# Cross-attention on one core: five instruction groups moved in the first rounds and in the tail

## The chip, the cores and the metric

The kernel runs on one core of a Trainium2 chip. The metric is the device time of one execution in microseconds (us). Five engines work side by side, each through its own instructions in order: TensorE (PE) multiplies matrices into PSUM, VectorE (DVE), ScalarE (ACT) and GpSimd (POOL) work element by element, and SyncE (SP) issues the DMA transfers. They wait for each other by semaphores.

## The reference

For each of 64 batches, with x of 256 rows by 512 and a context c of 256 rows by 384, all in float32:

```python
text_p = einsum('bld,dh->blh', x, W_text) + b_text
audio_p = einsum('bsd,dh->bsh', c, W_audio) + b_audio
Q = layer_norm(text_p, g1, beta1)
K = layer_norm(audio_p, g2, beta2)
alpha = softmax(einsum('blh,bsh->bls', Q, K) / sqrt(512))
H = einsum('bls,bsh->blh', alpha, audio_p)
H = einsum('blh,hk->blk', H, W_out) + b_out
out = layer_norm(H + x, g_out, beta_out)
```

## The kernel before

**What is computed how.** The kernel does the value projection last: alpha times c (the context, 256 by 384) times the product W_audio W_out, which it makes once (`fold_multiply`, `fold_evict`, `fold_bias`). The projections of the rounds use schemes with fewer products than a plain multiplication, and pay for it with sums. Class `Fork` (q, line 624) takes seven products of halves of W_text (`one` to `seven`), with the sums `xsum` of x made by POOL; class `Thirds` (k, and the output product `o` of a batch, line 516) cuts the rows of the weights in thirds, with the sums `csum` and `zsum` of c and z made by POOL and the sums `wa_thirds` and `wao_thirds` of the weights made once. `third_weights` (line 356) makes the latter in parts 0 to 4; in each a few sums of 128x171, on the engine that it is given. Part 2 is four sums; two of their results are weights of the products `four` and `five` of k. The results sit in PSUM, and steps such as `after_five` (DVE: a sum from one PSUM area to another, line 671) or `after_one` (ACT: a copy, line 654) stand between products: the next product adds to what they left.

Rows are turned into columns by a trip through memory outside the core: `store` writes rows, `fetch` reads them back as squares of 32 (`squares`, four DMAs, line 69), and DVE turns the squares (`turn`). This holds for q, k and for the exponentials e: `divide_e` (ACT, two instructions, line 743), `store_e`, `fetch_e`, `turn_e`.

**Order.** Everything is issued by hand in program order (`manual_schedule`), so each engine has exactly the order in which its calls stand, and SP the order of the loads, stores and fetches. Before the loop comes a start-up, in which batches 0 and 1 are projected and the weight sums are made (lines 1030 to 1106). Line 1079 gives parts 4 and 2 of the sums to DVE between `q[1].after_six()` and `q[1].after_five()` (line 1089); then come `turn_x(2)` (line 1090) and `q[1].rest()` (line 1095).

The loop at line 1112 has rounds b = 0 to 61. Round b loads the squares of c and x of batch b + 4 (`load_c`, `load_x`), projects batch b + 2 (`k2`, `q2`), scores batch b (`at`), takes the context of batch b - 1 (`last`), the output product of batch b - 2 (`old`) and the last layer norm of batch b - 3 (`settled`). The first rounds differ from the others: round 0 has no `last`, and round 1 does the softmax of batch 0 and later also that of its own batch. At the head of round 2 stand the loads of batch 6, among them the fetch of e of batch 1, and then the two loads of g_out and beta_out (`row`, line 118: one row of 512 to all 128 partitions, 256 KB). The division of e of batch 1 stands at the end of round 1 (lines 1324 and 1325), ahead of the copies of its context (`copy_one`, line 1327, and `copy_two` in round 2).

**The tail** (lines 1330 to 1430) finishes the last batches: `settled` is batch 59, `old` 60, `last` 61, `at` 62, `end` 63. Batches 62 and 63 take the output product plainly, in two tiles of 128 rows, three matmuls of 512 columns each (`multiply`, line 855). A tile then goes through `evict` (DVE, with statistics), `scale_soon` (DVE, and a power on POOL that gives the scale `rone`), `shift` (DVE: less the mean, times g_out) and `settle` (DVE: times the scale, plus beta_out). For batch 61 and for tile 0 of batch 63 the last step is instead `scale_row` on ACT and `lift_rows` on POOL, and the statistics come from `deviations` on ACT (squares, then POOL's power gives `rstd`). Tile 1 of batch 63 goes in halves of 256 columns (`multiply_halves`, `evict_halves`, `settle_halves`), each half with its own store. All lines are those of the kernel before.

Of the kernel before, what the change touches and what calls it, by code (L numbers as in the profile page):

```python
# [15 lines left out]
P = 128  # L16
# [6 lines left out]
def kernel(  # L23
# [18 lines left out]
    nc = tc.nc  # L42
    ctx.enter_context(tc.manual_schedule())
    B, L, D = x.shape
    S, DA = c.shape[1:]
    H = w_text.shape[1]
    LT, ST = L // P, S // P
    DC, AC, HC = D // P, DA // P, H // P
# [4 lines left out]
    H2 = H // 2  # L53
# [15 lines left out]
    def squares(dst, src):  # L69

        v = src.rearrange("(b j) (q f) -> q j b f", j=SQ, q=NQ)
        for q in (0, 2, 1, 3):
            nc.sync.dma_start(dst[q * SQ : (q + 1) * SQ], v[q])
# [7 lines left out]
    def load_c(b):  # L81
        cq = blk.tile([P, S // SQ, DA // NQ], F32, tag="cq", name=f"cq_{b}")
        squares(cq, c[b])
        blocks[b] = [cq]

    def load_x(b):
        xq = blk.tile([P, L // SQ, D // NQ], F32, tag="xq", name=f"xq_{b}")
        squares(xq, x[b])
        blocks[b].append(xq)
# [40 lines left out]
    wa_sb = const.tile([P, AC, H], F32, tag="wa", name="wa")  # L130
# [87 lines left out]
    def bias_parts():  # L218

        part = once.tile([P, D], F32, tag="e", name="part")  # L220
        nc.vector.scalar_tensor_tensor(
            part, wo_sb[:, 0, :], bac_sb[:, 0:1], bo_sb, ALU.mult, ALU.add
        )
        return part
# [8 lines left out]
    wao_sb = const.tile([P, AC, D], F32, tag="wao", name="wao")  # L233
# [15 lines left out]
    def fold_evict(a):  # L249
        nc.scalar.copy(wao_sb[:, a, :], folds[a])  # L250
# [7 lines left out]
    def moments(mv, src, t):  # L258

        st = small.tile([P, 6], F32, tag="st", name="st")  # L260
        nc.vector.bn_stats(st, src)
        nc.vector.bn_aggr(mv[:, t, :], st)
# [93 lines left out]
    def third_weights(w_sb, t, parts=(0, 1), engine=nc.gpsimd):  # L356

        b = [[w_sb[:, c, j : j + W3] for j in starts] for c in range(3)]
        w = {n: t[:, i, :W3] for i, n in enumerate((10, 4, 5, 1, 6, 2, 8, 9, 0, 3, 7))}
        w.update({14: b[2][0], 13: b[1][2], 11: b[0][0], 12: b[0][2]})  # L360
        plus = lambda o, i0, i1: engine.tensor_tensor(o, i0, i1, ALU.add)
        less = lambda o, i0, i1: engine.tensor_tensor(o, i0, i1, ALU.subtract)
        if 0 in parts:
            plus(w[0], b[1][1], b[1][2])
            less(w[6], w[0], b[2][0])
            less(w[2], b[1][0], w[0])
            plus(w[0], b[0][0], b[1][0])
            less(w[8], w[2], w[0])
        if 3 in parts:
            plus(w[0], w[0], b[1][2])  # L370
            less(w[9], b[1][2], b[2][0])
            less(w[7], b[0][1], b[0][0])
            plus(w[7], w[7], b[0][2])
        if 1 in parts:
            less(w[3], b[2][1], b[2][0])
            less(w[10], w[3], b[0][2])
        if 4 in parts:
            plus(w[4], w[3], b[2][2])
            plus(w[3], b[0][2], b[2][0])
            plus(w[3], w[3], b[2][2])  # L380
        if 2 in parts:
            less(w[5], b[2][0], b[2][1])
            less(w[5], w[5], b[1][2])
            less(w[1], w[5], b[1][1])
            less(w[1], w[1], b[0][1])
        return w
# [9 lines left out]
    def rstd_of(var, n, total=False):  # L396

        ve = small.tile([P, n], F32, tag="ve", name="ve")
        if total:
            nc.gpsimd.tensor_scalar(ve, var, 1.0 / D, EPS, ALU.mult, ALU.add)  # L400
        else:
            nc.gpsimd.tensor_scalar(ve, var, EPS, None, ALU.add)
        r = small.tile([P, n], F32, tag="rstd", name="rstd")
        nc.gpsimd.tensor_tensor(r, ve, nhalf[:, :n], ALU.pow)  # L404
        return [r[:, t : t + 1] for t in range(n)]
# [289 lines left out]
    class Attention:  # L695
# [138 lines left out]
                    junk, self.y[:, t, :], AF.Identity, scale=-1.0 / D, accum_out=self.nm[:, t : t + 1]  # L834
                )

        def deviations(self, lo=0, n=LT):

            for t in self.summed:
                junk = work.tile([P, D], F32, tag="junk", name="junk")  # L840
                nc.scalar.activation(  # L841
                    junk,
                    self.y[:, t, :],
                    AF.Square,
                    bias=self.nm[:, t : t + 1],
                    accum_out=self.ssq[:, t : t + 1],
                )
            self.r = dict(zip(self.summed, rstd_of(self.ssq[:, lo : lo + n], n, total=True)))
# [48 lines left out]
        def moments(self, tiles=range(LT)):  # L897
            if 0 in tiles:
                self.mv = small.tile([P, LT, 2], F32, tag="mvy", name="mvy")
            for t in tiles:  # L900
                moments(self.mv, self.y[:, t, :], t)
            if LT - 1 in tiles:
                self.scales()

        def multiply_halves(self, t, banks):
            self.ps_h = []
# [67 lines left out]
    def turn_x(b):  # L974
        xT = work.tile([P, DC, L], F32, tag="xT", name=f"xT_{b}")
        turn(xT, blocks[b][1], DC)
        return xT
# [12 lines left out]
    q, k, xT, cT, xs, cs, att = {}, {}, {}, {}, {}, {}, {}  # L990
    bank = third + fork
# [77 lines left out]
    wa_t = const.tile([P, 11, WP], F32, tag="wa_thirds", name="wa_thirds")  # L1069
# [6 lines left out]
    fold_multiply(1, 0, 2)  # L1076
    q[1].six()
    q[1].after_six()
    third_weights(wa_sb, wa_t, [4, 2], nc.vector)
    fold_evict(0)  # L1080
    Thirds.seed_with(ba_sb)
    k[1].normalise()
# [5 lines left out]
    q[1].five()  # L1088
    q[1].after_five()
    xT[2] = turn_x(2)  # L1090
    part = bias_parts()
    bias_rest(part, 1, 3)
    folds.append(p_at.tile([P, H], F32, tag="at", name="ps_fold"))
# [18 lines left out]
    for b in range(B - 2):  # L1112
        at = att[b] = att.get(b) or Attention(b)
        settled, old, last = att.pop(b - 3, None), att.get(b - 2), att.get(b - 1)
        three = b + 3 < B
        if b + 4 < B and b != 1:
            load_c(b + 4)
            if b == 2:
                last.fetch_e()
            load_x(b + 4)  # L1120
        if b == 2:
            go_sb = row(g_out, "go")
            beo_sb = row(beta_out, "beo")
        if b == 0:
            Fork.seed()
        k2 = k[b + 2] = Thirds("k", b + 2, cs.pop(b + 2), wa_blocks, ba_sb, ba_delta)
        if b < 3:
# [46 lines left out]
        q2.after_seven()  # L1174
        if b == 1:
            last.divide_e()
        if b < 3:
            at.affine_keys()
        else:
            at.affine_keys(2, 3)  # L1180
# [139 lines left out]
            last.context_one()  # L1320
        if three and old:
            k2.seed()
        if three and b:
            at.divide_e()
            at.store_e()
        if last and three:
# [2 lines left out]
    settled, old, last = att[B - 5], att[B - 4], att[B - 3]  # L1329
    at = att[B - 2]  # L1330
# [33 lines left out]
    end = Attention(B - 1)  # L1364
# [33 lines left out]
    last.o.leave_plus(x_rows[B - 3], lambda: None)  # L1398
    end.transpose_e(bank[5])
    end.copy_e()  # L1400
    at.multiply(1, bank[4])
    at.settle(0)
    last.totals()
    last.deviations()
    at.evict(1)
    at.scale_soon(1)
    at.shift(1)
    end.context()
    last.shift(0)
    last.shift(1)  # L1410
    at.settle(1)
    at.store()
    end.start_output()
# [6 lines left out]
    end.evict(0, stats=False)  # L1420
    end.statistics(0, 1)
    end.evict_halves(1, [0])
    end.shift(0)
    end.scale_row(0)
    end.evict_halves(1, [1])
    end.scale_soon(1)
    end.lift_rows(0, 1)
    end.shift(1)
    end.settle_halves(1)
    end.store(0, 1)  # L1430


# [30 lines left out]
```

## Time and profile before

| | |
|---|---|
| time, median of 3 runs | 1371.05 us (1370.75 to 1374.13) |
| the profiled execution, its own time | 1370.49 us |
| its span, first to last instruction | 1368.7 us |
| granted TensorE clock, mean | 0.999 |
| instructions | 26400 |
| DVE busy | 1112.9 us (81%) |
| ACT busy | 1090.0 us (80%) |
| POOL busy | 1159.8 us (85%) |
| DMA | 322.02 MB, mean 235 GB/s |

How to read the views that follow. A row of the timeline has the start and the duration in us, the engine, the line of the kernel, the operation, what it writes and reads with shapes, how many instructions were merged, and in brackets for how long the engine had been idle before it and which work ended that. `SPq` is the issue of a DMA, not its transfer. A matmul in float32 shows as two instructions per product. A row of the waits has the waiting engine, tile and line, the releaser, the total in us, the number of waits and the longest. A row of the stretches has the stretch, its length, the busy time of PE, PE's weight loads, DVE, ACT and POOL with the number of instructions, the granted clock, the busy share of the DMA engines and what they moved in GB/s.

### The profile page before, as it was taken

Reading aid. Unit: us, or ns where it says so; the run is one execution under the profiler, and the core shown is the slowest. Engines: PE = TensorE matmul, PEld = TensorE weight load, DVE = VectorE, ACT = ScalarE, POOL = GpSimd, SP = SyncE. Lnnn points to the kernel's source line nnn. Section 1 sums busy time; section 2 is a strip of 40 time slices with the busy share of each in tenths; the row PEclk is TensorE's granted clock in tenths of the full one; section 3 lists DMA queues with packets and bytes.
Section 4 is the critical chain, followed back from the end, with each engine's and each line's share of the span. In section 5 each row is a group of like instructions: output and inputs, shape, how many; then the busy total and the mean of one; then the engine's idle time right before and its main releaser. Section 6 shows DMA issues by size and latency. Waiting matters only on the chain. (4 is left out here: it accounts for less than half of the span.)

```text
span 1368.7 us, 26400 instructions
## 1 busy us (share of the span) xinstructions
PE 1356.2 (99%) x7423; PEld 1239.6 (91%) x7423; DVE 1112.9 (81%) x2688; ACT 1090.0 (80%) x2689; POOL 1159.8 (85%) x1928
## 2 busy tenths in 40 slices
PE   9999999999999999999999999999999999999997
PEld 5789999999999999999999999999999999999995
DVE  6778888888888888888888888888888888888868
ACT  5678888888788788888788887887887888888884
POOL 5788888888888888888888888888888888888866
PEclk9999999999999999999999999999999999999999
DMA  9788988988887889788779888798888888798762
GB/s 218 212 230 240 264 244 237 241 246 232 250 241 239 246 238 248 224 251 245 237 238 249 235 236 250 233 236 245 245 241 239 242 251 233 237 245 228 221 221 103
DMA packets 449096, 322.02 MB, mean 235 GB/s; under 512 B 153781, under 2 KB 381621, under 8 KB 448950
## 3 DMA queue, kind: packets, MB, share of 16 engines
q1 hardware_dynamic: 448854, 320.20, 82.3%
q8 instruction: 60, 0.98, 0.3%
q14 instruction: 86, 0.70, 0.2%
q10 hardware_dynamic: 96, 0.13, 0.0%
HBM read 203.57 MB, written 116.65 MB: 234 GB/s over the span
## 5 line engine op out<-in xcount | busy, mean ns | idle before, releaser
L712 PE MATMUL ps_sc<-kT,qT 128*128 128x256 f32 x1024 | 260.9, 379 | 0.0
L340 POOL TENSOR_TENSOR zsum<-zsum,zT 128x256 f32<-128x256 f32 x305 | 191.9, 646 | 14.4
L712 PEld LDWEIGHTS ps_sc<-kT,qT 128*128 128x128 f32 x1024 | 186.3, 190 | 17.3 <-ACT zT L793 0.2
L778 PE MATMUL ps_z<-eT,c 128*128 128x256 f32 x768 | 186.2, 379 | 0.0
L644 PE MATMUL ps_f<-wtsum,xsum 128*128 128x256 f32 x756 | 184.5, 380 | 0.3 <-ACT ps_f L655 0.3
L340 POOL TENSOR_TENSOR csum<-csum,cT 128x256 f32<-128x256 f32 x310 | 173.0, 567 | 9.9
L778 PEld LDWEIGHTS ps_z<-eT,c 128*128 128x128 f32 x768 | 143.0, 190 | 17.0 <-issue 0.5
L966 POOL TENSOR_TENSOR yr<-yr,beo 128x512 f32<-128x512 f32 x122 | 153.2, 1277 | 3.4 <-ACT yr L962 3.4
L644 PEld LDWEIGHTS ps_f<-wtsum,xsum 128*128 128x128 f32 x756 | 137.9, 190 | 15.0 <-issue 0.7
L404 POOL TENSOR_TENSOR rstd<-ve,nhalf 128x2 f32<-128x2 f32 x192 | 136.7, 712 | 16.0
L340 POOL TENSOR_TENSOR zsum<-zT 128x256 f32<-128x256 f32 x122 | 73.5, 602 | 86.3 <-ACT zT L796 86.3
L505 ACT ACTIVATE qT<-qT,columns 128x256 f32<-128x256 f32 x256 | 139.1, 594 | 2.8 <-DVE qT L76 2.8
L505 ACT ACTIVATE kT<-kT,columns 128x256 f32<-128x256 f32 x256 | 139.2, 595 | 1.5 <-DVE kT L76 1.1
L644 PE MATMUL ps_f<-wt,xT 128*128 128x256 f32 x504 | 129.3, 379 | 0.0
L729 ACT ACTIVATE e<-ps_sc,nmx 128x256 f32<-128x256 f32 x128 | 59.5, 469 | 63.4 <-DVE nmx L722 63.4
L948 DVE SCALAR_TENSOR_TENSOR yr<-yr,nm,go 128x512 f32<-128x512 f32 x124 | 103.7, 838 | 0.9 <-ACT junk L841 0.9
L644 PEld LDWEIGHTS ps_f<-wt,xT 128*128 128x128 f32 x504 | 92.9, 190 | 10.5 <-issue 0.5
L514 DVE TENSOR_TENSOR ps_l<-ps_m,t 128x171 f32<-128x171 f32 x248 | 85.5, 345 | 17.0
L796 ACT COPY zT<-ps_z 128x256 f32<-128x256 f32 x64 | 23.8, 372 | 85.7 <-PE ps_z L778 85.7
L514 DVE TENSOR_TENSOR ps_f<-ps_f,s 128x256 f32<-128x256 f32 x126 | 54.4, 432 | 46.0 <-PE ps_f L644 43.3
L841 ACT ACTIVATE junk<-yr,nm 128x512 f32<-128x512 f32 x124 | 87.9, 712 | 2.8 <-POOL nm L822 2.8
L962 ACT ACTIVATE yr<-yr,rstd 128x512 f32<-128x512 f32 x122 | 87.3, 717 | 2.1 <-POOL rstd L404 1.3
(247 smaller groups left out, 3775.7 us busy)
## 6 DMA issues: line engine op xcount, KB each, us to landing
kd<-kr SPq DMA_DIRECT2D x64, 512.0 KB, 2.9
kq<-kd SPq DMA_DIRECT2D x256, 128.0 KB, 3.1
qd<-qr SPq DMA_DIRECT2D x64, 512.0 KB, 2.9
qq<-qd SPq DMA_DIRECT2D x256, 128.0 KB, 2.7
xq<-in_x_dram SPq DMA_DIRECT2D x252, 128.0 KB, 3.2
x<-in_x_dram SPq DMA_DIRECT2D x63, 512.0 KB, 4.7
out_dram<-yr SPq DMA_DIRECT2D x62, 512.0 KB, 3.9
cq<-in_ctx_dram SPq DMA_DIRECT2D x252, 96.0 KB, 3.3
```

Of the source, the lines that this page charges most:

```text
L340: nc.gpsimd.tensor_tensor(*step)
L404: nc.gpsimd.tensor_tensor(r, ve, nhalf[:, :n], ALU.pow)
L505: nc.scalar.activation(self.T[:, k, :], self.T[:, k, :], AF.Identity, bias=bet[:, k : k + 1], scale=gam[:, k : k + 1],)
L514: nc.vector.tensor_tensor(o, i0, i1, op)
L644: nc.tensor.matmul(place, lhsT=side, rhs=w, start=False, stop=True, skip_group_check=True)
L712: nc.tensor.matmul(self.sc[:, t, :], lhsT=self.q.T[:, k, bass.ts(t, P)], rhs=self.k.T[:, k, :], start=(k == 0), stop=(k == HC - 1),)
L729: nc.scalar.activation(self.e[:, t, :], self.sc[:, t, :], AF.Exp, bias=self.nmx[:, t : t + 1], accum_out=self.den[:, t : t + 1],)
L778: nc.tensor.matmul(ps, lhsT=c_rows[self.b][:, s, bass.ts(j, P)], rhs=self.eT[:, s, :], start=(s == 0), stop=(s == ST - 1),)
L841: nc.scalar.activation(junk, self.y[:, t, :], AF.Square, bias=self.nm[:, t : t + 1], accum_out=self.ssq[:, t : t + 1],)
L948: nc.vector.scalar_tensor_tensor(row, row, self.nm[:, t : t + 1], go_sb, ALU.add, ALU.mult)
L962: nc.scalar.mul(self.y[:, t, :], self.y[:, t, :], self.r[t])
L966: nc.gpsimd.tensor_tensor(self.y[:, t, :], self.y[:, t, :], beo_sb, ALU.add)
```

## The change

Five groups of instructions move or take another form; what is computed stays.

1. Part 2 of the weight sums stands behind `turn_x(2)` instead of ahead of `after_five`.
2. `divide_e` and `store_e` of batch 1 stand in round 2 behind `after_seven`, no longer at the end of round 1; the loads of batch 6, with the fetch of that e between them, follow them there.
3. g_out and beta_out are loaded at the head of round 0 instead of round 2.
4. In the tail the second tile of batch 62 is multiplied in halves of 256 columns (`multiply_half`, new: three matmuls each), one ahead of and one behind the context of batch 63. The copies of that context stand ahead of and between the two instructions of `last.deviations`. `last.shift(0)` stands ahead of `at.evict(1)`, `last.shift(1)` between `at.scale_soon(1)` and `at.shift(1)`.
5. At the very end tile 0 of batch 63 is shifted and settled on DVE, behind the shift of tile 1, and stored ahead of the halves of tile 1; `scale_row` and `lift_rows` of that tile are gone.

```diff
-        def deviations(self, lo=0, n=LT):
+        def deviations(self, lo=0, n=LT, between=None):
             for t in self.summed:
+                if t and between:
+                    between()
...
+        def multiply_half(self, t, bank, h):
+            self.ps_y[t] = bank
+            for k in range(AC):
+                nc.tensor.matmul(
+                    bank[:, bass.ts(h, H2)],
+                    lhsT=self.zT[:, k, bass.ts(t, P)],
+                    rhs=wao_sb[:, k, bass.ts(h, H2)],
+                    start=(h == 0 and k == 0),
+                    stop=True,
+                    skip_group_check=True,
+                )
...
-    third_weights(wa_sb, wa_t, [4, 2], nc.vector)
+    third_weights(wa_sb, wa_t, [4], nc.vector)
...
     q[1].after_five()
     xT[2] = turn_x(2)
+    third_weights(wa_sb, wa_t, [2], nc.vector)
...
-        if b + 4 < B and b != 1:
+        if b + 4 < B and b not in (1, 2):
             load_c(b + 4)
-            if b == 2:
-                last.fetch_e()
             load_x(b + 4)
-        if b == 2:
+        if b == 0:
             go_sb = row(g_out, "go")
             beo_sb = row(beta_out, "beo")
-        if b == 0:
             Fork.seed()
...
         q2.after_seven()
         if b == 1:
             last.divide_e()
+        if b == 2:
+            last.divide_e()
+            last.store_e()
+            load_c(b + 4)
+            last.fetch_e()
+            load_x(b + 4)
...
-        if three and b:
+        if three and b > 1:
             at.divide_e()
             at.store_e()
...
-    at.multiply(1, bank[4])
+    at.multiply_half(1, bank[4], 0)
     at.settle(0)
     last.totals()
-    last.deviations()
+    end.context_one()
+    end.copy_one()
+    for s in range(ST):
+        end.context_two(s)
+    last.deviations(between=end.copy_two)
+    at.multiply_half(1, bank[4], 1)
+    last.shift(0)
     at.evict(1)
     at.scale_soon(1)
+    last.shift(1)
     at.shift(1)
-    end.context()
-    last.shift(0)
-    last.shift(1)
     at.settle(1)
...
     end.evict_halves(1, [0])
-    end.shift(0)
-    end.scale_row(0)
     end.evict_halves(1, [1])
     end.scale_soon(1)
-    end.lift_rows(0, 1)
     end.shift(1)
+    end.shift(0)
+    end.settle(0)
+    end.store(0, 1)
     end.settle_halves(1)
-    end.store(0, 1)
```

## The prediction

> **What bounds the kernel now.** I read the page first, then the stretches of the span, the waits of TensorE, the chain that ended last, and the timelines around the edited places.
>
> ```profile
> PE 1356.2 (99%) x7423; PEld 1239.6 (91%) x7423; DVE 1112.9 (81%) x2688; ACT 1090.0 (80%) x2689; POOL 1159.8 (85%) x1928
> ```
>
> ```profile
> 200.00:1300.00 1100.00, 1100.00 (x6139) 1023.01 (x6138) 908.57 (x2218) 899.12 (x2221) 957.39 (x1589) 1.00 0.84 240
> ```
>
> ```profile
> PE ps_f L644 <- DVE ps_f L514: 1.3, 1, 1.3
> PE ps_m L858 <- ACT zT L793: 0.5, 1, 0.5
> ```
>
> ```profile
> 1363.09 1.47 DVE y L940
> ```
>
> PE is busy 1356.2 us of 1368.7, and all of the 1100 us between 200 and 1300 (second row, first engine column). The rounds in the middle are bound by TensorE without a gap, and they issue the same work in the same order after the change. So the change can only reach the 12.5 us in which PE is idle: waits among the first rounds (1.3 us behind DVE, and two of 0.3 and 0.2 shown below), 0.5 behind ACT in the tail, and the time behind PE's last matmul, where the chain ends on DVE's settle of the last halves. All four waits gone and a tail some 1.5 us shorter make less than 4 us. A difference of 0.3%, about what a measurement of this kernel can tell from no change, is 4.1 us.
>
> **Part 1: weight sums behind after_five and the turn of x.**
>
> ```profile
> 36.92 0.61 DVE L362 TENSOR_TENSOR wa_thirds<-wa 128x171 f32<-128x171 f32 x1
> 37.56 1.49 DVE L362 TENSOR_TENSOR wa_thirds<-wa_thirds,wa 128x171 f32<-128x171 f32 x3
> 38.97 0.42 DVE L514 TENSOR_TENSOR ps_f<-ps_f,s 128x256 f32<-128x256 f32 x1
> 49.37 0.42 DVE L514 TENSOR_TENSOR ps_f<-ps_f,bt_step 128x256 f32<-128x256 f32 x1
> ```
>
> ```profile
> 36.29 1.88 PE L241 MATMUL ps_fold<-wo,waT 128*128 128x512 f32 x4
> 39.44 1.13 PE L644 MATMUL ps_f<-wt,xsum 128*128 128x256 f32 x4 [1.27 <-DVE ps_f L514]
> 50.20 1.03 PE L644 MATMUL ps_f<-wtsum,xsum 128*128 128x256 f32 x4
> ```
>
> ```profile
> 40.00:50.00 10.00, 10.00 (x48) 7.99 (x47) 9.28 (x18) 5.83 (x14) 5.89 (x9) 1.00 0.70 205
> ```
>
> PE's product q[1].rest (39.44) waits for DVE's after_five (38.97), and ahead of that on DVE stand the four sums of part 2, from 36.92 to 38.97: 2.05 us. Behind the move after_five starts at about 36.95 and ends by 37.4; PE is through with the products at 36.29 at about 38.1. So the whole stall goes: 1.27 us idle and some 0.2 of slower issue around it, 1.45.
>
> What is late next: DVE. It has the same work as before and hardly a pause, in order, up to after_six of batch 2 (ends 49.37 + 0.42 = 49.79), and PE's product at 50.20 needs that result. In 40 to 50 DVE is busy 9.28 of 10 us, so idle 0.72, nearly all of it before 49.79. PE can come earlier there by its slack of 0.41, less 0.1 for the signal, plus 0.6 of that idle time: 0.9. The rest of the 1.45 comes back as small waits of PE at about 44 and 49. Behind 50 DVE has room (5.95 busy in 50 to 60, below), and the gain stays. The moved sums are first used by the products near 49, 8 us after they are made, and the turn of x comes earlier: nothing else waits. Bounds: 0.3, if none of DVE's idle time lies on this path, to 1.45, if its sums run faster at their new place (they took 0.50 to 0.61 each in the rows). I take 0.9, from the row of DVE's idle time.
>
> **Part 2: the division of round 1 behind the copies of round 2.**
>
> ```profile
> 76.57 1.03 PE L644 MATMUL ps_f<-wt,xT 128*128 128x256 f32 x4
> 78.74 1.10 PE L644 MATMUL ps_f<-wtsum,xsum 128*128 128x256 f32 x4 [0.28 <-ACT ps_f L655]
> ```
>
> ```profile
> 76.66 0.91 ACT L743 ACTIVATE e<-e,rden 128x256 f32<-128x256 f32 x2
> 78.19 0.41 ACT L655 COPY ps_f<-ps_f 128x256 f32<-128x256 f32 x1
> 83.64 0.30 ACT L583 COPY u<-ps_u 128x171 f32<-128x171 f32 x1 [1.81 <-PE ps_u L530]
> ```
>
> ```profile
> 81.94 0.40 SPq L747 DMA_DIRECT2D ed<-e  x1
> ```
>
> ACT did the two divisions at 76.66, then two copies of zT, then the copy of R (78.19 to 78.60), for which PE's product six waited until 78.74. With 0.91 us less ahead of it, that copy waits only for PE's product one, done at 77.60, and is over by 78.0; six follows seven at 78.3 without a wait. Gain 0.45: 0.28 idle and the slowed issue around it. The divisions come back behind the next copy, and end before 80; ACT's affines run up to 0.9 later, into the 1.81 us for which ACT sat idle before 83.64. Without that cover the copies at 83.64 would be up to 0.9 late. Queued behind the divisions on SP is the store of e; it was issued at 81.94, and so is not held up by a division that ends at 80. The loads of c and x of batch 6 and the fetch of e follow it in the same order as before. Bounds: 0.28, the idle time alone, to 0.45; I take 0.45.
>
> **Part 3: rows of g_out and beta_out loaded in round 0.**
>
> ```profile
> 52.14 1.87 SPq L73 DMA_DIRECT2D xq<-in_x_dram  x4
> 58.99 0.38 SPq L476 DMA_DIRECT2D qd<-qr  x1
> 61.85 1.84 SPq L73 DMA_DIRECT2D qq<-qd  x4
> 90.06 0.43 SPq L120 DMA_DIRECT2D beo<-in_L_xattn_beta_out_dram  x1
> 92.46 0.37 SPq L476 DMA_DIRECT2D qd<-qr  x1
> 100.30 1.81 SPq L73 DMA_DIRECT2D qq<-qd  x4
> ```
>
> ```profile
> 107.56 0.71 DVE L498 STREAM_TRANSPOSE kT<-kq 128x512 f32<-128x512 f32 x1 [0.74 <-DMA kq<-kd]
> ```
>
> ```profile
> 110.15 0.53 PE L530 MATMUL ps_u<-wao_thirds,zsum 128*128 128x171 f32 x2 [0.23 <-DVE ps_u L514]
> ```
>
> ```profile
> 50.00:60.00 10.00, 10.00 (x55) 9.15 (x54) 5.95 (x11) 9.12 (x24) 6.82 (x15) 1.00 0.56 133
> ```
>
> In round 2 the two row loads (256 KB each) stood on SP just ahead of two tile loads and the store of q (92.46). The fetch that needs this store came 7.84 us after it (100.30); in round 0 it came after 2.86 (58.99 to 61.85). Then DVE waited 0.74 us for k's squares (107.56), and behind that its sum, for which PE waited at 110.15, was late: 0.23 idle, about 0.4 with the slowed issue. At the 240 GB/s of the middle of the span, 512 KB less in front are 2.2 us, more than the 0.74: the wait goes. In round 0 the loads are issued at 54.0 (52.14 + 1.87), when SP has nothing to do until 58.99 and the DMA engines are busy at 0.56 and 133 GB/s; the same 2.2 us put them through before the store. Bounds: 0, if the wait stays, to 0.4, all of it; I take 0.4.
>
> **Part 4: the tail.** The product of batch 62's second tile goes in halves around the last context; the last batch's first tile is settled on DVE alone.
>
> ```profile
> 1348.79 2.74 PE L858 MATMUL ps_f<-wao,zT 128*128 128x512 f32 x6
> ```
>
> ```profile
> 1352.59 0.72 ACT L841 ACTIVATE junk<-yr,nm 128x512 f32<-128x512 f32 x1 [2.82 <-POOL nm L822]
> 1354.02 0.56 ACT L793 COPY zT<-ps_z 128x512 f32<-128x512 f32 x1
> ```
>
> ```profile
> 1354.80 1.41 DVE L948 SCALAR_TENSOR_TENSOR yr<-yr,nm,go 128x512 f32<-128x512 f32 x2
> 1356.65 0.75 DVE L957 SCALAR_TENSOR_TENSOR y<-y,rone,beo 128x512 f32<-128x512 f32 x1 [0.44 <-POOL rone L887]
> 1357.52 0.75 DVE L867 SCALAR_TENSOR_TENSOR y<-ps_m,rden,x 128x512 f32<-128x512 f32 x1
> 1358.81 0.48 DVE L925 SCALAR_TENSOR_TENSOR y<-ps_l,rden,x 128x256 f32<-128x256 f32 x1 [0.54 <-PE ps_l L911]
> 1359.96 0.75 DVE L948 SCALAR_TENSOR_TENSOR y<-y,nm,go 128x512 f32<-128x512 f32 x1 [0.21 <-ACT junk L841]
> 1363.09 1.86 DVE L940 SCALAR_TENSOR_TENSOR y<-y,rone,beo 128x256 f32<-128x256 f32 x2 [0.43 <-POOL rone L887]
> ```
>
> ```profile
> 1356.94 2.83 POOL L966 TENSOR_TENSOR yr<-yr,beo 128x512 f32<-128x512 f32 x2 [0.32 <-ACT yr L962]
> 1363.03 1.25 POOL L966 TENSOR_TENSOR y<-y,beo 128x512 f32<-128x512 f32 x1
> ```
>
> ```profile
> 1365.51 0.40 SPq L969 DMA_DIRECT2D out_dram<-y  x1
> ```
>
> PE does half the product (1.3 of 2.6 us), the context from 1350.1, and the other half until 1354.0. ACT copies z at 1352.0, not at 1354.02, so PE's wait of 0.5 goes. But PE does not set the end here, DVE does. It now shifts row 0 of batch 61 first, which waits for ACT's squares (1352.59 + 0.72 = 1353.31), then evicts the product at 1354.2, and after the same instructions as before (statistics, two shifts) settle(1) of batch 62 is up at 1357.35, 0.7 later than at 1356.65.
>
> There POOL comes in. Before, POOL's sum at 1356.94 waited for ACT's scaled row, and settle(1), which waits only for rone, had begun. Now row 0 is shifted by 1354.1 instead of 1355.5, ACT has scaled it by 1356.2, and POOL goes from rone straight on to the sum, ahead of settle(1). What that costs is seen at 1363.03: POOL's sum of 1.25 us began 0.06 ahead of DVE's settle, and a half that needs 0.47 took 1.47. So settle(1) ends near 1359.1, and end.evict(0) starts at 1359.05 instead of 1357.52: 1.55 later. The nearest row without such a delay is the pair of shifts at 1354.80, 0.7 each while POOL worked on its rstd; by it end.evict(0) starts at 1358.05. I go by 1363.03, where POOL's operation is the same.
>
> The Trainium skill, "SBUF — State Buffer", section "Who interferes with whom", has a rule for it: a VectorE instruction with two SBUF inputs and a GpSimd instruction that reads SBUF shut each other out, and the one that starts first keeps the port. By it settle(1) waits and the parts sum to 2.2; without it they sum to 3.2. The row at 1363.03 agrees.
>
> Behind end.evict(0) the new order is shorter. Before, the last store was issued 8.0 us after it (1357.52 to 1365.51). Out of these fall 1.0 behind POOL's sum, DVE's waits of 0.54, 0.21 and 0.43 (its three rows with brackets), and 0.55 for which the store of row 0 came after the last half (1363.09 + 1.86 = 1364.95). In comes DVE's settle(0), 0.7. That leaves 6.0, and the tail gains 8.0 - 6.0 - 1.55 = 0.45. Bounds: 1.45 without POOL's hold; -0.25 if POOL's last rone is shut out during one more whole-row operation of DVE (0.7).
>
> **The sum:** 0.9 + 0.45 + 0.4 + 0.45 = 2.2 us. The profiled execution took 1370.49 (1.8 around its span), so it would take 1368.3; the median of the runs shown, 1371.05, is 0.56 above it, so 1368.8 there, which I predict.
>
> **The rivals.**
> - POOL does not get ahead of settle(1). For: the pair at 1354.80. Against: 1363.03. The tail gives 1.45, the sum 3.2: 1367.8. Chance 0.19.
> - DVE becomes the bound of round 0 and gives most of part 1 back. For: 9.28 of 10 us busy. Against: it does have idle time. Part 1 gives 0.3, the sum 1.6: 1369.4. Chance 0.16.
> - The tail doesn't do what the edit says: end.evict(0) 1.55 late and rone shut out once more. Sum 1.5: 1369.5. Chance 0.11.
> - Slower: the row loads are still in the DMA queue when round 0 stores q. In round 2 the way from that store to its fetch was 5.0 us longer than in round 0 (7.84 against 2.86). If 61.85 comes 5 us later, the fetch of e of round 0 behind it on SP does too, and PE's first context product waits for that e: up to 5.0, less the 2.2, so 2.8 slower: 1373.8. It decides as soon as PE is held up there by over 2.2 us. Against it: 5 us of a free SP, and DMA engines at 0.56. Chance 0.08.
>
> **How the numbers follow.** The forecast has 0.46. The range goes from 1366.6 to 1371.6: the upper bounds give 1.45 + 0.45 + 0.4 + 1.45 = 3.75, so 1367.3, the lower ones 0.3 + 0.28 + 0 - 0.25 = 0.33, so 1370.7, each with 0.7 to 0.9 for the spread of the runs shown (1370.75 to 1374.13). It leaves out the last rival and little else. Faster by over 0.3% needs over 4.1 us, all upper bounds and a lucky run: 0.09. Slower by over 0.3% needs the last rival at its worst, or something not seen: 0.08. Within 0.3%: 0.83.
>
> **What would show it.** After the change: no wait of PE for after_five near 38, small ones near 44 or 49 instead; none for the copy of R near 77; no wait of DVE for k's squares near 106, and none of PE behind it; the row loads on SP near 53. In the tail settle(1) of batch 62 at 1.3 us or more beside POOL's sum, end.evict(0) later and the last store earlier (by 0.45) than before, both against the first rounds' gain. I am wrong if PE is idle past round 3, or waits for a fetch in rounds 0 and 1.

## The result, and the profile after

The changed kernel takes **1369.17 us** (median of 14 runs, 1367.89 to 1371.05) beside 1371.74 us for the kernel before in the same comparison (14 runs, 1370.60 to 1374.13): a ratio of 0.9981, 95% interval 0.9973 to 0.9989, so 2.6 us faster (1.5 to 3.7). The prediction was 1368.8, or 2.2 us less. The profiled execution took 1368.85 us (span 1367.1, mean granted clock 0.998), where the working had given 1368.3.

Busy time of each engine, from the page, and TensorE's waits, from the view of the waits:

```profile
PE 1355.5 (99%) x7429; PEld 1241.0 (91%) x7429; DVE 1113.6 (81%) x2689; ACT 1089.9 (80%) x2688; POOL 1158.6 (85%) x1927
```

```profile
PE ps_f L184 <- POOL ones L108: 1.5, 1, 1.5
PE ps_z L778 <- DVE eT L76: 1.1, 1, 1.1
```

All four waits behind DVE and ACT that the prediction counted are gone. The first row, 1.5 us, is the wait of the start-up that was there before. The second row is new.

TensorE's timeline of the first rounds shows both. This start-up is 0.28 us later than that of before (the fold product near 36 us stands at 36.57 against 36.29), so distances from that product are compared.

```profile
36.57 1.88 PE L241 MATMUL ps_fold<-wo,waT 128*128 128x512 f32 x4
38.28 1.03 PE L644 MATMUL ps_f<-wt,xsum 128*128 128x256 f32 x4
48.98 1.03 PE L644 MATMUL ps_f<-wtsum,xsum 128*128 128x256 f32 x4
72.52 1.99 PE L778 MATMUL ps_z<-eT,c 128*128 128x256 f32 x8 [1.14 <-DVE eT L76]
77.53 1.89 PE L644 MATMUL ps_f<-wtsum,xsum 128*128 128x256 f32 x8
109.33 0.45 PE L530 MATMUL ps_u<-wao_thirds,zsum 128*128 128x171 f32 x2
```

q[1].rest (38.28) follows the fold product without a gap. The product near 50 stands 12.41 us behind that fold product (48.98 - 36.57), where it was 13.91 before (50.20 - 36.29): 1.50 gained, not 0.9. Product six at 77.53 and the product at 109.33 don't wait, as forecast. But the first context product waits 1.14 us at 72.52 for e's turned squares. The place is that of the slower rival, below the 2.2 us from which that rival would have decided. But the prediction also named a wait for a fetch in rounds 0 and 1 as a sign that it is wrong. This is such a wait, in round 1, and the sum has no term for it.

DVE and POOL in that stretch, and SP:

```profile
34.93 0.33 DVE L361 TENSOR_TENSOR wa_thirds<-wa_thirds,wa 128x171 f32<-128x171 f32 x1
35.29 0.74 DVE L361 TENSOR_TENSOR wa_thirds<-wa 128x171 f32<-128x171 f32 x1
36.77 0.43 DVE L514 TENSOR_TENSOR ps_f<-ps_f,s 128x256 f32<-128x256 f32 x1
38.27 0.35 DVE L362 TENSOR_TENSOR wa_thirds<-wa 128x171 f32<-128x171 f32 x1
```

```profile
34.98 3.03 POOL L340 TENSOR_TENSOR csum<-csum,cT 128x256 f32<-128x256 f32 x5
```

```profile
54.42 0.44 SPq L120 DMA_DIRECT2D beo<-in_L_xattn_beta_out_dram  x1
57.77 0.38 SPq L476 DMA_DIRECT2D qd<-qr  x1
61.95 1.81 SPq L73 DMA_DIRECT2D qq<-qd  x4
64.36 1.92 SPq L73 DMA_DIRECT2D kq<-kd  x4
91.22 0.37 SPq L476 DMA_DIRECT2D qd<-qr  x1
97.05 1.80 SPq L73 DMA_DIRECT2D qq<-qd  x4
```

The first of the moved sums takes 0.35 us at its new place (38.27), 0.61 before; the other three 1.45 and 1.49 together. The one at 34.93 began just ahead of POOL's five sums of c (34.98 to 38.0) and took 0.33; the one at 35.29, in the midst of them, took 0.74; the moved ones stand behind them. DVE is through earlier, and none of the small waits of TensorE near 44 or 49 that the prediction expected shows here. On SP, the fetch of q in round 3 follows its store by 5.83 us (91.22 to 97.05; 7.84 before), as wanted. In round 0 it follows by 4.18 (57.77 to 61.95; 2.86 before).

The tail, against a first-round gain of 1.12 us (batch 62's first settle stands at 1350.56, before at 1351.68). The lines are the changed kernel's: L971 is `settle`, L869 `evict`, L980 `lift_rows`, L925 the last batch's halves on TensorE, L957 the stores of those halves:

```profile
1356.36 1.57 DVE L971 SCALAR_TENSOR_TENSOR y<-y,rone,beo 128x512 f32<-128x512 f32 x1
1357.86 0.74 DVE L869 SCALAR_TENSOR_TENSOR y<-ps_m,rden,x 128x512 f32<-128x512 f32 x1
```

```profile
1355.97 3.09 POOL L980 TENSOR_TENSOR yr<-yr,beo 128x512 f32<-128x512 f32 x2
```

```profile
1356.72 1.46 PE L925 MATMUL ps_u<-wao,zT 128*128 128x256 f32 x6
```

```profile
1363.38 0.87 SPq L957 DMA_DIRECT2D out_dram<-y  x2
```

Settle(1) takes 1.57 us beside POOL's sum (forecast "1.3 us or more"); end.evict(0) is 1.46 later than before once the 1.12 is taken out (forecast 1.55). The last of the two stores in the row at 1363.38 starts at about 1363.82, so 0.57 earlier in the same sense (1365.51 - 1363.82 - 1.12; forecast 0.45).

So the sum came true, with one term too small (1.50 for 0.9) and a wait of 1.14 against it. The experiments ask which of these figures belongs to the program and which to this one execution.

### The profile page after: what moved, and what is told of

The parts are those of the page before. It is cut to its first block, busy times and chain, and to the rows that moved or that the text cites. A ratio compares the mean times of both kernels' runs of the same rounds, so it can differ in the third digit from the quotient of the medians.

```text
span 1367.1 us, 26408 instructions
## 1 busy us (share of the span) xinstructions
PE 1355.5 (99%) x7429; PEld 1241.0 (91%) x7429; DVE 1113.6 (81%) x2689; ACT 1089.9 (80%) x2688; POOL 1158.6 (85%) x1927
## 5 line engine op out<-in xcount | busy, mean ns | idle before, releaser
L980 POOL TENSOR_TENSOR yr<-yr,beo 128x512 f32<-128x512 f32 x122 | 153.6, 1281 | 3.1 <-ACT yr L976 3.1
L311 POOL TENSOR_TENSOR xsum<-xT 128x256 f32<-128x256 f32 x124 | 88.2, 733 | 0.0
```

The lines of the kernel that those rows point to most:

```text
L311: self.engine.tensor_tensor(*step)
L980: nc.gpsimd.tensor_tensor(self.y[:, t, :], self.y[:, t, :], beo_sb, ALU.add)
```

## The experiments

**Theory A** for the wait at 72.5: the two row loads, now in round 0, hold up q's store and with it the fetches behind it. **Theory B**: the fetch of e is where it always was, and TensorE, 1.5 us earlier, only waits longer there. In the expectations of the first three runs below, A is the theory and B the rival. All comparisons below are with the kernel before on the same chip; differences in us are the ratio times 1371.

### Part 3 undone

```diff
         if b == 0:
-            go_sb = row(g_out, "go")
-            beo_sb = row(beta_out, "beo")
...
         if b == 2:
...
             load_x(b + 4)
+            go_sb = row(g_out, "go")
+            beo_sb = row(beta_out, "beo")
```

> The changed kernel with its part 3 undone: the two row loads (g_out, beta_out) stand in round 2 again, behind the loads of batch 6. Theory (the two loads hold up round 0's store of q, and behind it the fetches of q and e): TensorE's wait of 1.14 us for e's turned squares near 72.5 us is gone (under 0.1), the fetch of q in round 0 again follows its store by about 2.9 us instead of 4.2, and in round 3 VectorE's wait for k's squares and TensorE's stall near 110 come back (0.2 to 0.4 us). Net about 0.7 to 0.8 us faster than the changed kernel, near 1368.4 where that is 1369.2. Rival (TensorE arrives 1.5 us earlier from part 1, and the fetch of e has not moved): the wait near 72.5 stays at 0.8 us or more, and the kernel is 0.3 to 0.4 us slower than the changed one.

1370.17 us (11 runs), ratio 0.9992 (0.9983 to 1.0001): 1.1 us faster than before, not the 0.7 better than the changed kernel that theory A wanted. The fetch of q does follow its store by 2.86 us again. TensorE's timeline:

```profile
71.77 2.00 PE L778 MATMUL ps_z<-eT,c 128*128 128x256 f32 x8 [0.43 <-DVE eT L76]
109.22 0.53 PE L530 MATMUL ps_u<-wao_thirds,zsum 128*128 128x171 f32 x2 [0.48 <-DVE ps_u L514]
117.86 0.82 PE L530 MATMUL ps_n<-wa,csum 128*128 128x171 f32 x4 [0.91 <-DVE yr L614]
```

The wait for e is 0.43, between the two theories. The stall of round 3 is back, and larger than in the profile of before: 0.48 and 0.91 instead of 0.23.

### Each part alone

Part 3 alone on the kernel before (the diff's lines for `row`):

> The kernel before with part 3 alone: the two row loads in round 0. Theory (the loads hold up the fetch of e): TensorE waits for e's turned squares near 73.5 us in the kernel before's time, for 1 us if the transfer had no slack there, less by whatever slack it had; the stall of round 3 goes; net between 0.4 faster and 0.8 slower than the kernel before. Rival (the wait needs part 1's earlier TensorE): no wait near 73.5, stall of round 3 gone, 0.4 us faster.

1369.62 us (11 runs), ratio 0.9991 (0.9982 to 1.0000): 1.2 us faster. No wait for e, and no stall in round 3. Theory A's lag does not show either: the fetch of q follows its store by 2.86 us with the row loads ahead of it.

```profile
54.05 0.43 SPq L120 DMA_DIRECT2D beo<-in_L_xattn_beta_out_dram  x1
58.52 0.38 SPq L476 DMA_DIRECT2D qd<-qr  x1
61.38 2.46 SPq L73 DMA_DIRECT2D qq<-qd  x4
```

Part 1 alone (`third_weights` 2 behind `turn_x(2)`):

> The kernel before with part 1 alone: the weight sums behind the turn of x. Measured in the changed kernel's trace, TensorE is 1.5 us earlier near 50 us. Theory (the later wait for e comes from the row loads): no wait near 72, all of the 1.5 us stays, 1.45 us faster than the kernel before. Rival (the wait comes from the earlier TensorE): a wait for e near 72 of 0.8 us or more, and net under 0.7 us faster. The forecast's own figure for this part was 0.9 us, with small waits of TensorE near 44 and 49: if it holds they show here.

1370.68 us (11 runs), ratio 0.9995 (0.9987 to 1.0004): 0.7 us faster. In its trace TensorE, then DVE and POOL:

```profile
44.98 1.10 PE L255 MATMUL ps_bias<-part,ones 128*128 128x512 f32 x2 [0.61 <-DVE part L229]
72.86 1.99 PE L778 MATMUL ps_z<-eT,c 128*128 128x256 f32 x8 [0.30 <-DVE eT L76]
77.87 1.93 PE L644 MATMUL ps_f<-wtsum,xsum 128*128 128x256 f32 x8
112.21 0.53 PE L530 MATMUL ps_u<-wao_thirds,zsum 128*128 128x171 f32 x2 [2.34 <-DVE ps_u L514]
```

```profile
43.55 1.28 DVE L229 SCALAR_TENSOR_TENSOR part<-wo,columns,part 128x512 f32<-128x512 f32 x1
43.56 1.86 POOL L311 TENSOR_TENSOR xsum<-xT 128x256 f32<-128x256 f32 x2
```

Here is the small wait near 44 that the prediction expected: DVE's operation at 43.55 takes 1.28 us (0.74 at the same place in the changed kernel), TensorE waits 0.61 for it, and part 1 is worth 0.6 us up to the product near 50. Here POOL's sums of x begin together with that operation (43.56). The wait for e is 0.30: theory B wanted 0.8 or more. TensorE does not wait for the copy of R (77.87, products seven and six in one row), though the division stands where it was before. And round 3 stalls for 2.34 us.

The tail alone (points 4 and 5 of the change):

> The kernel before with the tail (parts 4 and 5 of the change) alone. Theory: the tail is 0.45 to 0.55 us shorter than before, settle of batch 62's second tile takes 1.5 us or more beside GpSimd's sum, and the eviction of the last batch's first tile comes 1.45 to 1.55 us later than before. Rival (tail worth nothing): the last store is issued within 0.2 us of before's 1365.5. Rival (the tail's 0.5 us needs the earlier first rounds): not possible with TensorE busy without a gap in between, so the same tail shows here shifted in time by 1.1 us.

1370.45 us (11 runs), ratio 0.9996 (0.9987 to 1.0005). Its rounds are those of the kernel before, and yet TensorE waits for e:

```profile
73.57 1.99 PE L778 MATMUL ps_z<-eT,c 128*128 128x256 f32 x8 [0.87 <-DVE eT L76]
```

```profile
61.94 3.06 SPq L73 DMA_DIRECT2D qq<-qd  x4
65.59 1.92 SPq L73 DMA_DIRECT2D kq<-kd  x4
```

This row shows that neither theory is the whole cause: 0.87 us of wait with neither the row loads nor the earlier TensorE. SP took 3.06 us to issue the four fetches of q, 1.84 in the profile of before, and everything behind them on SP was later. Round 3 does not stall in this execution. In the tail, with a shift of 0.13 (batch 62's first settle at 1351.81), end.evict(0) is 1.45 later and the last store some 0.58 earlier than before.

Part 2 alone (the diff's lines for `divide_e` and `store_e`, with the row loads left behind the loads of batch 6):

> The kernel before with part 2 alone: the division of round 1 behind the copies of round 2; the row loads stay in round 2 behind the loads of batch 6. Theory: TensorE's wait for the copy of R near 78.7 is gone, ScalarE's later affines hold nothing up, 0.28 to 0.45 us faster than the kernel before, too little for the time alone to show. In round 3, where the row loads still stand ahead of q's store, TensorE stalls again between 105 and 120 us, as in the kernel before and in the looks at the weight sums alone and at the changed kernel with its rows in round 2 (0.2 to 2.3 us); no stall there speaks for a mere accident. Rival (ScalarE's affines become late): a new wait of TensorE for ScalarE between 80 and 92 us.

1371.44 us (11 runs), ratio 1.0004 (0.9995 to 1.0013). TensorE does not wait for the copy of R, and ACT brings up no new wait. That alone does not show the mechanism, since TensorE came 0.66 us late, held by e; and 0.3 to 0.45 us is below what the time can show. Round 3 stalls for 2.07 us:

```profile
112.38 0.53 PE L530 MATMUL ps_u<-wao_thirds,zsum 128*128 128x171 f32 x2 [2.07 <-DVE ps_u L514]
```

### The cost doubled

Two more row loads behind the two of round 2, in the kernel before:

```diff
             beo_sb = row(beta_out, "beo")
+            row(g_out, "go2")
+            row(beta_out, "beo2")
```

> The kernel before, with the suspected cost doubled: behind the two row loads of round 2 stand two more of the same kind, into tiles that nothing reads, 512 KB more in front of q's store. Theory (the row loads hold up q's store and the fetches behind it, and TensorE stalls in round 3 for that): the fetch of q in round 3 follows its store by about 10 us instead of 7.7 to 9.1, VectorE waits 2 to 3 us for k's squares, TensorE stalls 1.5 to 3 us between 105 and 120 us, and the kernel is 1 to 2.2 us slower than the kernel before. Rival (the stall of round 3 comes from other transfers and varies by itself): the stall stays within the 0 to 2.3 us that four looks with the loads in round 2 have shown, and the time within 0.5 us of the kernel before.

**1377.12 us** (5 runs), ratio 1.0043 (1.0031 to 1.0056): 5.9 us slower, far over the 1 to 2.2 expected. SP, TensorE, and the stretches of the span (the columns after PE's: weight loads, DVE, ACT, POOL, granted clock, DMA share, GB/s):

```profile
95.03 2.21 SPq L476 DMA_DIRECT2D qd<-qr  x1
105.65 1.81 SPq L73 DMA_DIRECT2D qq<-qd  x4
```

```profile
114.67 0.91 PE L530 MATMUL ps_u<-wao_thirds,zsum 128*128 128x171 f32 x2 [4.65 <-DVE ps_u L514]
```

```profile
96.00:98.00 2.00, 2.00 (x14) 1.88 (x13) 1.90 (x8) 0.72 (x2) 0.51 (x2) 1.00 1.06 103
98.00:100.00 2.00, 2.00 (x12) 1.80 (x11) 1.64 (x4) 1.62 (x5) 1.09 (x2) 1.00 0.98 132
...
114.60:117.00 2.40, 2.33 (x6) 2.08 (x7) 1.56 (x4) 0.37 (x1) 2.24 (x4) 0.50 1.01 207
117.00:120.00 3.00, 3.00 (x11) 2.74 (x10) 0.12 (x1) 0.00 (x0) 2.61 (x3) 0.50 0.95 225
120.00:122.00 2.00, 2.00 (x12) 1.95 (x11) 1.83 (x4) 0.00 (x0) 0.00 (x0) 0.84 0.97 368
122.00:125.00 3.00, 3.00 (x18) 2.72 (x17) 2.63 (x12) 2.37 (x8) 0.00 (x0) 1.00 0.63 232
```

The direction is theory's: the fetch of q follows its store by 10.62 us and TensorE stalls 4.65. Two things make it dearer. SP is held up while it issues: the store of q takes 2.21 us (0.37 without the loads), at a time when the DMA engines are full at 103 and 132 GB/s. And behind the long stall the granted clock is 0.50 for some 6.0 us: the 5.4 us of the two rows with 0.50, and some 0.6 of the next row, whose 0.84 is a mean. At half the clock that is an estimated cost of 3.0 us. Stall and clock make 7.6, less the 0.2 of stall before: 7.4, and the profiled execution took 7.5 more (1377.96 against 1370.49).

The Trainium skill, "TensorE: Matmul & The Clock Gate", section "Part 1: The HAM clock gate", says that TensorE falls to half its clock after an idle window of about 3.4 us. The traces here agree: 0.50 behind 4.65 us, and 1.00 behind the stalls of 2.34 and 2.07 us.

### The tail's lock

Batch 62's settle(1) reads beta_out from PSUM, in the changed kernel:

```diff
     last.deviations(between=end.copy_two)
+    nc.scalar.copy(bank[3], beo_sb)
...
-    at.settle(1)
+    at.settle(1, bank[3])
```

> The changed kernel, with one edit in the tail: ScalarE copies beta_out into a free PSUM area, and the settle of batch 62's second tile reads it there, so that this VectorE operation has one SBUF input instead of two. Its first rounds are those of the changed kernel, so this is also a second look at them. Theory (GpSimd's sum of beta_out shuts VectorE out): the settle takes 0.75 us instead of 1.57, the eviction of the last batch's first tile comes 0.7 to 0.8 us earlier against the end of TensorE's work, and the time falls by up to 0.8 us. Rival (the settle is late or slow for another reason, such as its wait for rone or the store): it still takes over 1.3 us, and nothing else moves. First rounds: if TensorE's wait for e near 72.5 us belongs to the changed program, it is there again with 0.9 to 1.3 us and the fetch of q again follows its store by 4.2 us; if it is a matter of the single execution, it differs by more than 0.4 us.

1367.84 us (9 runs), ratio 0.9975 (0.9965 to 0.9984). DVE, TensorE, SP and POOL:

```profile
1356.03 0.75 DVE L971 SCALAR_TENSOR_TENSOR y<-y,rone,ps_n 128x512 f32<-128x512 f32 x1
1356.70 0.74 DVE L869 SCALAR_TENSOR_TENSOR y<-ps_m,rden,x 128x512 f32<-128x512 f32 x1
```

```profile
1356.36 1.46 PE L925 MATMUL ps_u<-wao,zT 128*128 128x256 f32 x6
```

```profile
1362.22 0.88 SPq L957 DMA_DIRECT2D out_dram<-y  x2
```

```profile
1355.61 2.65 POOL L980 TENSOR_TENSOR yr<-yr,beo 128x512 f32<-128x512 f32 x2
```

With one SBUF input the settle takes 0.75 beside the same sums of POOL, and the two sums take 2.65 instead of 3.09. Against TensorE's last product, end.evict(0) is at 0.34 instead of 1.14 (1357.86 - 1356.72), and the last stores at 5.86 instead of 6.66: 0.80 us, as expected. The lock is shown. The wait for e, in the same rounds as the changed kernel's, is 0.26, and the fetch of q follows its store by 2.86: both figures of the changed profile were that execution's own.

Batch 62's second tile on ACT and POOL instead:

```diff
-    at.settle(1)
-    at.store()
+    at.store(0, 1)
...
     last.lift_rows()
     last.store()
+    at.scale_row(1)
+    at.lift_rows(1, 1)
+    at.store(1, 1)
```

> The changed kernel, with batch 62's second tile scaled on ScalarE and given beta_out on GpSimd, behind those of batch 61, instead of settled on VectorE. First rounds as in the changed kernel (a third look). Theory (VectorE's chain sets the end, and the settle costs it 1.5 us with GpSimd beside it): the eviction of the last batch's first tile comes 1.4 to 1.55 us earlier, and the last store 0.5 to 1.5 us earlier, depending on how long GpSimd's extra sum of about 1.5 us shuts out VectorE's shifts behind it or delays the last rone. Rival (GpSimd becomes the bound of the tail): the last rone comes later and the last store is issued no earlier than in the changed kernel.

1368.04 us (9 runs), ratio 0.9976 (0.9966 to 0.9986). end.evict(0) comes 1.69 us earlier (1355.04, ahead of TensorE's last product at 1355.59), more than the 1.4 to 1.55 expected, but the last stores only 0.66 (6.00 behind it instead of 6.66):

```profile
1360.37 0.75 DVE L971 SCALAR_TENSOR_TENSOR y<-y,rstd,beo 128x512 f32<-128x512 f32 x1 [0.45 <-POOL rstd L404]
1361.04 0.88 DVE L954 SCALAR_TENSOR_TENSOR y<-y,rone,beo 128x256 f32<-128x256 f32 x2
```

DVE now waits 0.45 for POOL's rstd, which stands behind POOL's extra sum: there POOL has become the bound, as the rival said, though the last store is still earlier, which the rival denied. No wait for e in this profile.

### e ahead of q and k

```diff
             last.store_e()
-            k[2].fetch()
+            q[2].fetch()
             last.fetch_e()
+            k[2].fetch()
...
+        if b == 1:
+            last.turn_e()
+            k[2].turn([0])
         k[b + 1].turn([1])
```

(q's fetch is no longer issued at the end of round 0, and e and the first half of k no longer turned at their old places in round 1.)

> The changed kernel, with e of batch 0 ahead of batch 2's q and k in the queues: its store is issued ahead of q's fetch, its fetch ahead of k's, and VectorE turns it ahead of k's two halves. Theory (TensorE's wait near 72.5 us is e's way through SP's queue and VectorE's order behind the fetches of q and k, so that a TensorE that is earlier only waits longer there): the wait is gone, TensorE's first context product starts at 71.4 or earlier, and TensorE is 0.8 to 1.2 us earlier near 117 than in the changed kernel, minus what k's later turn brings back as a wait of round 2 (none expected, since k of batch 2 is used there from about 77). Net about 1 us faster than the changed kernel. Rival (the row loads' transfers hold it, and e's data are late whatever the order): the wait stays over 0.7 us.

1368.46 us (10 runs), ratio 0.9976 (0.9967 to 0.9985). No wait for e, but the first context product stands at 72.32, not at 71.4 or earlier: the product near 50 came 13.16 us behind the fold product in this execution, not 12.41. With the ACT tail beside it:

> Both edits at once: e of batch 0 ahead of q and k of batch 2, and batch 62's second tile on ScalarE and GpSimd. If both theories hold, the two gains add up, since TensorE is busy without a gap between them: 1.5 to 2.5 us faster than the changed kernel, near 1367. If either falls, the sum is that of the other one alone.

1367.69 us (8 runs), ratio 0.9974 (0.9964 to 0.9984). No wait for e either, but TensorE waits 0.61 in round 2 (at 89.53, for POOL's sums of c): part of the gain comes back there. At 3.6 us faster than before, some 1.0 beyond the changed kernel, it falls short of the 1.5 to 2.5 expected.

### The version that the runs point to, and the changed kernel again

The settle from PSUM and e ahead of q and k together, with the edits shown above:

> The version that the runs so far point to: the changed kernel with batch 62's settle reading beta_out from PSUM (measured: the last store 0.8 us earlier against TensorE's last product) and with e of batch 0 ahead of batch 2's q and k (measured: no wait for e). If both hold, no wait for e near 72, settle at 0.75 us, and about 1.2 us faster than the changed kernel beside it, so 3.8 us faster than the kernel before, near 1367.4; if the order of e is worth nothing on average, 0.8 us faster than the changed kernel.

**1367.01 us** (6 runs), ratio 0.9970 (0.9957 to 0.9982): 4.1 us faster than before, and 1.5 less than the changed kernel on the same chip, though the two intervals overlap. No wait for e, settle at 0.75; but again a wait in round 2, 0.86, behind DVE, which had itself waited 1.37 us for the next squares of k (at 85.28):

```profile
87.86 0.53 PE L530 MATMUL ps_u<-wao_thirds,zsum 128*128 128x171 f32 x2 [0.86 <-DVE ps_u L514]
```

In the rows the new order of e gains nothing in sum: from the fold product near 36 us to batch 62's first settle the three profiles with it take 1314.1 us in the mean, the four with the changed first rounds and e in its old place 1313.4. The times are 0.3 to 0.7 us better with it, less than the intervals. So what the order of e is worth stays open; the 0.8 of the settle is what the rows show.

The changed kernel, unedited:

> The changed kernel itself once more, on the chip of the runs beside it: 2.6 us faster than the kernel before within 1 us, and another look at the first rounds. If TensorE's wait for e is a matter of the single execution (0, 0.26 and 1.14 us in the three looks at this program so far), it lies anywhere between 0 and 1.2; the stall of round 3 is absent again, because the row loads no longer stand ahead of it.

1368.50 us (11 runs), ratio 0.9980 (0.9971 to 0.9989). Its waits, from the same view as above, are one row of the start-up:

```profile
PE ps_f L184 <- POOL ones L108: 1.5, 1, 1.5
```

## Why the prediction was right, and where it was not

Fourteen profiles show the first rounds. The table has, in us, each number the difference of two starts or the bracket of a wait:

- *to 50*: from the fold product near 36 us to the product near 50;
- *q to k*: from the store of q to the fetch of k in round 0, on SP;
- *e*: TensorE's wait for e;
- *q to q*: from the store of q to its fetch in round 3;
- *stall*: TensorE's waits in round 3 and just behind it (105 to 120 us).

| kernel | part 1 in | rows in round | to 50 | q to k | e | q to q | stall |
|---|---|---|---|---|---|---|---|
| before | no | 2 | 13.91 | 5.29 | 0 | 7.84 | 0.2 |
| tail alone | no | 2 | 13.75 | 6.51 | 0.87 | 7.66 | 0 |
| division alone | no | 2 | 13.96 | 6.44 | 0.66 | 9.07 | 2.1 |
| weights alone | yes | 2 | 13.32 | 6.13 | 0.30 | 9.07 | 2.3 |
| rows back in round 2 | yes | 2 | 12.43 | 6.17 | 0.43 | 8.16 | 1.4 |
| rows doubled | no | 2 | 13.49 | 6.08 | 0.31 | 10.62 | 4.7 |
| rows alone | no | 0 | 13.60 | 6.27 | 0 | 5.85 | 0 |
| changed | yes | 0 | 12.41 | 6.59 | 1.14 | 5.83 | 0 |
| changed again | yes | 0 | 12.43 | 5.83 | 0 | 5.18 | 0 |
| settle from PSUM | yes | 0 | 13.14 | 6.41 | 0.26 | 5.42 | 0 |
| settle on ACT | yes | 0 | 12.45 | 5.69 | 0 | 4.00 | 0 |
| e first | yes | 0 | 13.16 | - | 0 | 3.76 | 0 |
| e first, ACT | yes | 0 | 13.34 | - | 0 | 6.29 | 0 |
| PSUM, e first | yes | 0 | 12.54 | - | 0 | 7.15 | 0 |

- **Part 1 (0.9): the mean met, in part by luck.** The way to 50 has a mean of 13.74 in the five profiles without it and 12.80 in the nine with it: 0.94. But no profile shows 0.9. Against that mean, or the 13.91 of before, five gain 1.2 to 1.5, near the upper bound of 1.45, and four 0.4 to 0.8. In the four, DVE's operation near 43.5 takes 1.28 instead of 0.74, and TensorE waits 0.4 to 0.6 for it. POOL's sums of x begin 0.01 us behind the start of that operation in these four, and 0.3 or more behind it in all others. That looks like the lock of the tail, but no run here tests it. The prediction had the loss from DVE's idle time as a whole; the rows put it at this one operation.
- **Part 2 (0.45): the mechanism right, the size too large on average.** From the first context product of round 1 to that of round 2 TensorE takes 21.73 to 21.75 us with the division moved, the two profiles with the stalls of 0.61 and 0.86 in round 2 left out. With the division in its old place it takes 22.26 in the profile of before and 22.02 with the rows alone, where TensorE came unheld, and 21.75 to 21.80 with the tail alone, the weights alone and the rows doubled, where it came late from its wait for e. So the stall was worth 0.5, 0.3 and next to nothing three times, 0.2 in the mean: a stall that another one covers has no price of its own.
- **Part 3 (0.4, bounds 0 to 0.4): the step that failed, as a size.** The prediction took the stall of round 3 from one profile, 0.23 us and 0.4 with the slow issue around it, and made that the upper bound. With the row loads in round 2 (not doubled) the stall is 0.2, 0, 2.1, 2.3 and 1.4, a mean of 1.2; with them in round 0 it is 0 in eight of eight, and the way from q to q is 5.4 in the mean instead of 8.4. The time does not contradict it: 1.2 us for part 3 alone (0 to 2.5), and 1.5 between the changed kernel and the same with its rows back (2.6 less 1.1, each with an interval of over 1 us to either side). That the loads are the cause is shown by doubling them: 10.6 from q to q, a stall of 4.7, 5.9 us. Why the stall is small or large is not shown. The two small ones are those with the first rounds of before; each of the three large ones has part 1 or part 2 in its kernel. With the weights alone the order from round 0 on is that of before, and still it stalls 2.3. What goes with it is the time on SP from beta_out's load to the store of q: 2.4 and 2.1 us where the stall is small, 1.5 in the three others. Another 0.2 us of part 3 stands where the prediction saw nothing to gain, in the middle: there three rounds take 20.88 to 20.90 us in the six kernels with the rows in round 2, and 20.79 in the eight with them in round 0, for a reason that no run here shows.
- **The slower rival (row loads ahead of q's store in round 0): not seen as such.** The wait for e has a mean of 0.28 with the rows in round 0 (five profiles with e in its old place) and 0.43 in the six with them in round 2; with and without part 1 it is 0.36 and 0.37. So it is neither theory A nor theory B. What it goes with is SP's way from q to k: no wait up to 5.83, 0 to 0.43 from 6.08 to 6.41, 0.66 to 1.14 from 6.44. In the program DVE turns e only behind k, and with e ahead of k the wait is gone in three of three. Why SP takes 1.8 us to issue the same four fetches in one execution and 3.1 in another was not settled. The changed kernel's 4.18 us from the store of q to its fetch did not come back in three more profiles of the same rounds (2.86, 2.93, 3.14).
- **Part 4 (0.45): right in each link.** Settle(1) 1.57 beside POOL, end.evict(0) 1.46 later, the last store 5.96 behind it (forecast 6.0), the end 0.57 earlier, and 0.58 with the tail alone. The Trainium skill's rule on the shared port ("SBUF — State Buffer", "Who interferes with whom"), by which the sum was 2.2 and not 3.2, is confirmed by the settle that reads PSUM: 0.75 and 0.80 us gained.
- **The sum: right, in part by luck.** From these means it is 0.94 + 0.2 + 1.2 + 0.57 = 2.9; measured 2.6 (1.5 to 3.7). The rows give it directly too. From the fold product near 36 us to batch 62's first settle the two profiles with the first rounds of before take 1315.3 us, the four with the changed ones 1313.4 (1312.8 to 1314.0): 1.9, and 2.5 with the tail. The forecast's 2.2 is near because its errors partly cancel: part 3 too small by up to 0.8, part 2 too large by some 0.25. The wait for e, for which the sum had no term, takes nothing from the gain only because the first rounds of before have it as well (0 and 0.87). The four parts alone measure 0.7, -0.5, 1.2 and 0.5 us, each with an interval of some 1.2 to either side, so that none is told from zero by its time alone (part 3's interval ends there); what tells them apart is the rows.

## What to carry to other kernels

A stall behind a transfer is one draw from a spread: before its row becomes a term of a sum, ask how far the same transfer varies, and let the bound reach beyond the profile at hand. A load that nobody needs yet is not free in front of a store that a round trip waits for; put it where no store is due. And when POOL is about to read SBUF beside a chain of DVE that sets the end, give DVE's second input another home, PSUM here: the last store came 0.80 us earlier by it, and 0.66 with the work given to ACT and POOL instead.

## What the runs showed of the hardware

- Behind two row loads the issue of q's store on SP took 0.37 to 1.2 us, behind four 2.2, and 0.37 without. Around that store the DMA engines were full (share 0.97 to 1.06) at only 96 to 132 GB/s, for 2 us in three profiles with two row loads and for 4 us with four; in the changed kernel the 4 us behind the store moved 309 and 402 GB/s at 1.01 and 1.04.
- The granted clock of TensorE fell to 0.50 behind an idle 4.65 us and stayed there for about 6 us of work; behind 2.34 us it stayed at 1.00.
- A DVE sum of 128x171 from SBUF took 0.34 us with POOL idle beside it and up to 0.88 among POOL's sums of c. DVE's operation near 43.5 took 0.74, or 1.28 where POOL's sums of x began with it.
- With DVE's second input in PSUM both engines gained: the settle took 0.75 instead of 1.57, and POOL's two sums beside it 2.65 instead of 3.09.
